# Eight row buffers, an addition ahead of the transposes and one store a chunk in the last stage of a two-layer model

## The chip, the cores and the metric

The kernel runs on one core of a Trainium2 chip. The metric is the time of one execution on the device, in microseconds (us); lower is better. Before the change three runs gave 2809.3, 2803.34 and 2809.07 us, median 2809.07. The core has five engines that run on their own and meet at semaphores: TensorE (PE: matmuls and transposes into PSUM), VectorE (DVE), ScalarE (ACT), GpSimd (POOL: here also indirect DMAs) and SyncE (SP: here the queue that issues nearly all plain DMAs).

## What is computed

The input is x, 64 sequences of 64 tokens with 256 features, 4096 tokens in all. Two layers add to it four times: a conditioned scan with attention, a quantized feed-forward, an RNN with a Mamba block, and last two mixtures of experts, one behind the other. The last term is what matters here:

```python
def _L1_ffn_ref(x, Wg, W1, W2, W3):
    xt = x.reshape(B * S, D)
    scores = xt @ Wg.T
    topk_scores, topk_idx = jax.lax.top_k(scores, TOP_K)      # 2 of 8 experts
    gate = jax.nn.silu(jnp.einsum('td,ehd->teh', xt, W1))
    up = jnp.einsum('td,ehd->teh', xt, W2)
    y = jnp.einsum('teh,edh->ted', gate * up, W3)
    ...
    out = jnp.einsum('te,ted->td', w, y)                      # sum of a token's two results
    return out.reshape(B, S, D)
...
x = x + _L1_ffn_ref(_L1_cond2_ref(...), L1_ffn_Wg, L1_ffn_W1, L1_ffn_W2, L1_ffn_W3)
```

Each token goes to two of eight experts, the results are weighted and added, and the sum is added to the residual x.

## The kernel before

The kernel keeps features on the 128 partitions (two blocks k of 128) and tokens along the free axis, and works in 8 chunks of 512 tokens (`NCH`, `CH`, `TT` = 4 groups of 128 tokens to a chunk).

The mixtures (function `mixtures`) don't compute all experts for all tokens. A gate chooses two experts for every token of a chunk (`Gate.chunk`, `Gate.lot`), and the token's row, 256 features and four tags, is sent by eight indirect DMAs a chunk (`Routing.send`, L1320, on POOL's queue) into the two experts' regions of a DRAM table. Expert tiles of 256 or 128 rows are then read back (`Routing.read`, L1328) with the expert's weights (L1520), both issued on SP. For the last mixture these are the tiles of class `Swiglu`, with two tiles loaded ahead and three buffers. A tile transposes its rows (L1534, copied by VectorE at L1536), makes the inner activations (matmuls L1661 and L1669, ScalarE L1664 and L1672, VectorE L1665 and L1674), multiplies by the last matrix (L1559), scales by the gate (ScalarE L1561), and gives each row's result to the place of its token and choice in another DRAM table, `ffn_y`, by indirect DMAs (`Routing.give`, L1335). VectorE takes a tile's tags apart in some small operations that begin at L1539. Its matmul outputs use four PSUM banks of one tag in rotation. After the gate's last chunk VectorE makes the tables that tell SP which rows and experts the remaining tiles are (`Routing.tiles`, from L1391 on).

In the last stage all results lie in `ffn_y`, two rows for each token. `Routing.fetch` (L1344) reads those of a chunk, 1 MiB, into a tile of 128 partitions x 4 groups x 2 results x 256 features. It waits for every indirect DMA that gave results. The residual x of the chunk lies in another tile, `x3_c`, loaded (L1993) while tiles were still running. For each of the two feature blocks TensorE transposes the eight 128x128 blocks of a chunk into one PSUM bank, and adds the second result of a token to the first there, in the accumulation (L2005). VectorE adds the bank to x (L2014), and SP stores the block (L2015), 256 KB. Rows have two buffers, `rows3_0` and `rows3_1`, and take 16 KB per partition of the pool `gx`; the eight x3 tiles take 32 KB.

A scheduler of the language's tile layer orders the instructions on each engine's queue, sets the semaphores, and gives pools their memory; a pool that is opened takes memory that earlier pools have given up, and its first writers wait for the last users. The order on SP can so change where a pool changes its size. SP issues DMAs in order: one that waits holds back those behind it.

Of the kernel before, what the change touches and what calls it, by code (L numbers as in the profile page):

```python
# [13 lines left out]
F32 = mybir.dt.float32  # L14
# [7 lines left out]
P = 128  # L22
B, L, D = 64, 64, 256
NT = B * L
CH = 512
NCH = NT // CH
KD = D // P
# [51 lines left out]
def bank(g, shape=(P, CH), dt=F32, tag="ps"):  # L79
    tag = g.tag or tag  # L80
    return g.psum.tile(list(shape), dt, tag=tag, name=tag)
# [1034 lines left out]
TT = CH // P  # L1116
# [345 lines left out]
def turns(queue):  # L1462

    while True:
        while queue and next(queue[0], END) is END:
            queue.popleft()
        yield
# [426 lines left out]
def mixtures(g, mix, x, weights, out, last, work, close):  # L1894

    nc, tc = g.nc, g.tc
    some = lambda pieces, n: deque(islice(pieces, n), 0)

    def tiles_on(tiles, n, *beside):

        at = 0
        for mark in tiles:
            n -= mark is TILE
            if n == 0:
                break  # L1910
            at += 1
            for pieces, many in beside:
                some(pieces, int(at * many) - int((at - 1) * many))

    with ExitStack() as ctx:
        pool = lambda name, bufs: ctx.enter_context(tc.tile_pool(name=name, bufs=bufs))
        p1 = pool("e1", 1)
        gate = Gate(g, p1, x)
        first, q2, q3, qy = pool("qw", Gelu.AHEAD + 1), pool("q2", 2), pool("q3", 2), pool("qy", 6)
        moe0, moe1 = mix.routings  # L1920
        n = moe0.ntl
        tables1 = []
        tiles = Gelu(g, (q2, q3, qy, first), weights[0]).run(
            [(moe0, lambda: mix.tables, n, NHT, None), (moe1, lambda: tables1[0], n, NHT, None)]
        )
        n += NHT
        next(tiles)
        others, shared = mix.rest(last, work, q3), mix.shared(NCH - 1, last, work)
        for _ in range(5):
            some(others, 1)  # L1930
            some(shared, 3)
        tiles_on(tiles, n - Gelu.AHEAD + 1, (others, 0.6), (shared, 0.8))
        some(others, None)
        some(shared, None)
        tables1.append(moe1.tiles(p1))
        close()

        pw, p2, p3, py = pool("gw", Swiglu.AHEAD + 1), pool("g2", 2), pool("g3", 3), pool("gy", 4)
        pg, close_pg = scoped(tc, "gate", side="right")
        pg2, close_pg2 = scoped(tc, "gate2", side="right", bufs=2)  # L1940

        def gates(chunks):
            got = {}

            def fetch(c):
                rows = pg.tile([P, TT, RW], F32, name=f"x2_{c % MLOT}")
                got[c] = rows, mix.fetch(c, rows[:, :, :D], pg2)

            fetch(chunks[0])

            for _ in range(4):
                yield
            for c in chunks:
                if c + 1 in chunks:
                    fetch(c + 1)
                    yield
                rows, routed = got.pop(c)
                mix.combine(rows[:, :, :D], routed)
                yield from gate.chunk(c, rows, pg, pg2)

        routing = gate.routing
        ntl = routing.ntl - EARLY
        tables2 = []
        tiles2 = Swiglu(g, (p2, p3, py, pw), weights[1]).run(
            [
                (routing, lambda: tables2[0], EARLY, 0, routing.sent),
                (routing, lambda: tables2[1], ntl, NHT, None),
            ]
        )

        tiles_on(tiles, Gelu.AHEAD + 3)
        others = gates(range(MLOT))
        sends = turns(gate.sends)
        tiles_on(tiles, n - 7, (others, 0.85), (sends, 0.42))
        some(others, None)
        some(chain.from_iterable(gate.sends), None)
        tables2.append(routing.early(p1))
        next(tiles2)
        some(tiles, None)
        others = gates(range(MLOT, NCH))  # L1980
        some(tiles2, 7)
        tiles_on(tiles2, EARLY - Swiglu.AHEAD, (others, 0.85), (sends, 0.42))
        some(others, None)
        some(chain.from_iterable(gate.sends), None)
        close_pg2()
        close_pg()
        tables2.append(routing.tiles(p1))
        px, close_px = scoped(tc, "gx", side="right")
        xs = []
        for c in range(NCH):  # L1990
            tiles_on(tiles2, 1)
            x = px.tile([P, KD, CH], F32, name=f"x3_{c}")
            nc.sync.dma_start(x, g.x[:, :, ts(c, CH)])  # L1993
            xs.append(x)
        some(tiles2, None)
        for c in range(NCH):
            rows = px.tile([P, TT, 2, D], F32, name=f"rows3_{c % 2}")
            routing.fetch(c, rows)
            x = xs[c]
            for k in range(KD):  # L2000
                po = bank(g, tag="acc")

                for t in range(TT):
                    for j in range(2):
                        nc.tensor.matmul(  # L2005
                            po[:, ts(t, P)],
                            rows[:, t, j, ts(k, P)],
                            g.ident,
                            start=(t == 0 and j == 0),
                            stop=(t == TT - 1 and j == 1),  # L2010
                            is_transpose=True,
                            skip_group_check=True,
                        )
                nc.vector.tensor_add(x[:, k, :], x[:, k, :], po)  # L2014
                nc.sync.dma_start(out[ts(k, P), ts(c, CH)], x[:, k, :])  # L2015
        close_px()


def scoped(tc, name, side=None, bufs=1):

    stack = ExitStack()
    kw = {"side": side} if side else {}
    return stack.enter_context(tc.tile_pool(name=name, bufs=bufs, **kw)), stack.close
# [3 lines left out]
def tile_adaln_attn_ffn_d2(ctx: ExitStack, tc: tile.TileContext, a: dict, out: bass.AP):  # L2027
# [49 lines left out]
    def close():  # L2077
        for one in (close_work, close_shared, close_mamba, close_hs):
            one()

    mixtures(g, mix, rows["ffn1"], weights, out, last, work, close)
    close_banks()
    close_mix()
# [79 lines left out]
```

## Time and profile before

| | |
|---|---|
| three runs | 2809.3, 2803.34, 2809.07 us |
| the profiled execution | 2806.4 us, span 2804.7 us |
| granted TensorE clock, mean of the span | 0.924 |
| busy share: PE, DVE, ACT, POOL | 84%, 64%, 49%, 47% |
| last results land in `ffn_y` | 2751.99 us |
| first fetch of rows issued, last addition ended | 2752.07, 2801.57 us |
| fetch of rows (L1344), 8 of 1024 KB, issue to landing | median 7.9 us |
| transposes (L2005), 128 | median 421 ns, weight loads 230 ns |
| addition to x (L2014), 16 of 128x512 | median 686 ns |
| store (L2015), 16 of 256 KB, issue to landing | 2.0 to 8.3 us, median 5.2 |
| loads of x3 (L1993), 8 of 512 KB | issued 2303.0 to 2338.8 us, 9.4 to 12.8 us to landing |

All times are from one execution recorded by the hardware profiler, in microseconds from the start of the span. In rows of the profile a line is named as L2005, `out<-in` are the program's tiles, `xN` counts instructions, and a bracket gives how long the engine was idle before and what released it. The chain of waits follows the work that ended last back in time. "PEld" are TensorE's weight loads, "SPq" is SP's issuing of a DMA.

### The profile page before, as it was taken

What the parts mean: (1) busy time and instruction counts of PE and PEld (TensorE: products, weight loads), DVE (VectorE), ACT (ScalarE), POOL (GpSimd) and SP (SyncE); (2) the same over time, 40 slices, a digit from 0 to 9 for tenths busy, and PEclk for the clock granted to TensorE, in tenths of its full rate; (3) what the DMA queues carried; (4) which work ended last, traced back from release to release, by engine and by line L of the source; (5) the groups of instructions that cost most, each with busy time, mean ns of one, the idle gap of its engine ahead of it and who ended that gap; (6) DMA issues with size and microseconds to landing.
All of it is one profiled execution on the core that took longest, in us unless ns stands there. A gap on an engine that the chain in (4) does not pass through costs nothing.

```text
span 2804.7 us, 34605 instructions
## 1 busy us (share of the span) xinstructions
PE 2368.8 (84%) x12072; PEld 1698.5 (61%) x12092; DVE 1783.4 (64%) x3017; ACT 1380.3 (49%) x2278; POOL 1323.8 (47%) x1158
## 2 busy tenths in 40 slices
PE   3979967998577888888778888869987999999995
PEld 3634435775245555555555555557765778888885
DVE  0467638982699889897978889883354443333332
ACT  0567627783675757676565757543332222222220
POOL 0013336540677676767586878754647341111110
PEclk9879988998768999998899899889999999999997
DMA  9999810002212122212122131314787757555545
GB/s 228 371 359 346 272 45 1 1 1 100 68 61 83 65 73 71 72 65 72 45 71 95 58 102 65 110 42 152 252 269 262 294 202 265 193 194 215 199 167 185
DMA packets 180630, 406.05 MB, mean 145 GB/s; under 512 B 24913, under 2 KB 84562, under 8 KB 175074
## 3 DMA queue, kind: packets, MB, share of 16 engines
q1 hardware_dynamic: 167010, 366.80, 38.7%
q0 software_dynamic: 13440, 36.98, 3.4%
q8 instruction: 97, 1.59, 0.2%
q14 instruction: 83, 0.68, 0.1%
HBM read 280.76 MB, written 144.98 MB: 152 GB/s over the span
## 4 chain that ended last, share of the span: by engine, by line
PE 45%; DVE 25%; issue 8%; ACT 7%; POOL 5%; DMA 3%; SPq 0%; DVEq 0%; POOLq 0%; ACTq 0%
DVE hb L1067 12%; PE ps L1661 11%; PE acc L1559 8%; PE out L446 4%; DVE hb L1069 3%; PE yp L1083 2%; PE mq L1797 2%; PE ps L1628 2%; PE mp L964 2%; DVE xc L909 2%; PE mq L1813 1%; PE acc L437 1%; PE s L412 1%; DVE h L628 1%; PE ps L1669 1%
## 5 line engine op out<-in xcount | busy, mean ns | idle before, releaser
L1028 POOL TENSOR_TENSOR hb<-dx,Bn 128x1024 f32<-128x1024 f32 x256 | 601.3, 2358 | 257.7 <-PE yp L1083 253.3
L1067 DVE TENSOR_TENSOR_SCAN hb<-dA,hb 128x512 f32<-128x512 f32 x512 | 602.5, 1208 | 32.4 <-ACT dA L1035 29.9
L1035 ACT ACTIVATE dA<-delta,A 128x504 f32<-128x504 f32 x512 | 344.4, 683 | 305.3 <-DVE hb L1067 302.7
L1083 PEld LDWEIGHTS yp<-ident,hb 128*128 128x128 f32 x2048 | 272.5, 154 | 179.2 <-issue 141.2
L1069 DVE TENSOR_TENSOR hb<-hb,cb 128x1024 f32<-128x1024 f32 x256 | 312.0, 1219 | 77.0 <-PE cb L980 59.5
L1661 PE MATMUL ps<-gxT,w 128*128 128x256 f32 (+1 forms) x1600 | 324.1, 361 | 0.8 <-DVE gxT L1536 0.8
L1083 PE MATMUL yp<-ident,hb 128*128 128x128 f32 x2048 | 307.6, 295 | 0.0
L1661 PEld LDWEIGHTS ps<-gxT,w 128*128 128x128 f32 x1600 | 276.4, 190 | 46.3 <-issue 12.4
L1797 PE MATMUL mq<-x,moe_s 128*128 128x256 f32 x896 | 254.6, 417 | 47.0 <-ACT up L1804 25.6
L1335 POOL DMA_INDIRECT ffn_y<-gy,to x72 | 69.2, 961 | 428.8 <-ACT gy L1561 416.3
L1797 PEld LDWEIGHTS mq<-x,moe_s 128*128 128x128 f32 x896 | 171.4, 207 | 109.8 <-ACT up L1804 34.1
L1665 DVE TENSOR_TENSOR gh<-gs,ps 128x256 f32<-128x256 f32 (+1 forms) x200 | 78.5, 393 | 205.3 <-ACT gs L1664 205.3
L980 PE MATMUL cb<-parts,pick 80*128 80x512 bf16 x256 | 106.5, 416 | 111.3 <-DVE hb L1069 96.5
L1559 PE MATMUL acc<-w,gh 128*128 128x256 f32 (+1 forms) x864 | 188.2, 388 | 0.0
L1664 ACT ACTIVATE gs<-ps 128x256 f32<-128x256 f32 (+1 forms) x200 | 72.4, 362 | 230.2 <-PE ps L1661 227.6
L1561 ACT ACTIVATE gy<-acc,wt 128x256 f32<-128x256 f32 x152 | 67.0, 472 | 234.1 <-PE acc L1559 229.6
L1559 PEld LDWEIGHTS acc<-w,gh 128*128 128x128 f32 (+1 forms) x864 | 145.4, 189 | 30.1 <-issue 13.4
L428 POOL TENSOR_TENSOR E<-E,z 128x1024 f32<-128x1024 f32 x32 | 61.6, 1924 | 151.9 <-DVE z L427 61.5
L446 PE MATMUL out<-oT,hs 128*128 128x512 f32 x256 | 119.5, 611 | 1.5 <-ACT oT L439 1.5
L1813 PE MATMUL mq<-moe_s,sh 128*128 128x256 f32 x448 | 114.3, 393 | 6.6 <-ACT up L1804 6.6
L1335 POOL DMA_INDIRECT moe_y<-gy,to x80 | 77.3, 966 | 68.2 <-ACT gy L1561 50.9
L1813 PEld LDWEIGHTS mq<-moe_s,sh 128*128 128x128 f32 x448 | 82.5, 194 | 40.5 <-issue 19.1
(459 smaller groups left out, 4376.6 us busy)
## 6 DMA issues: line engine op xcount, KB each, us to landing
w<-ffn_w SPq DMA_DIRECT2D x40, 2176.0 KB, 9.4
Bn<-B SPq DMA_DIRECT2D x128, 512.0 KB, 3.7
moe_x<-fill SPq DMA_DIRECT2D x130, 260.0 KB, 5.9
ffn_x<-fill SPq DMA_DIRECT2D x129, 260.0 KB, 6.0
w<-moe_w SPq DMA_DIRECT2D x48, 512.0 KB, 4.7
ffn_w<-in_ffn_W_dram SPq DMA_DIRECT2D x16, 640.0 KB, 8.3
gx<-moe_x SPq DMA_DIRECT2D x32, 260.0 KB, 5.0
gx<-ffn_x SPq DMA_DIRECT2D x32, 260.0 KB, 9.2
```

The costliest lines, as they stand in the source:

```text
L446: nc.tensor.matmul(ps, M[:, o, ts(k, P)], v.o[:, o], start=(o == 0), stop=(o == H // 2 - 1))
L980: nc.tensor.matmul(t, pick[:, n : n + 1].to_broadcast([rows, P]), v.parts, start=True, stop=True)
L1028: nc.gpsimd.tensor_mul(hb, vs[c].dx[p], Bn[:, n % NB, :].unsqueeze(1).to_broadcast([P, PI, CH]))
L1035: nc.scalar.activation(decays[s][i][:, :, 1:], seq(vs[c].delta[p][:, i, :])[:, :, 1:], AF.Exp, scale=w.A[:, p * PI + i, n : n + 1],)
L1067: ins = nc.vector.tensor_tensor_scan(h, dA[i].rearrange("p b l -> p (b l)"), h, 0.0, ALU.mult, ALU.add)
L1069: ins = nc.vector.tensor_tensor(hb, hb, cb.unsqueeze(1).to_broadcast([P, PI, CH]), ALU.mult)
L1083: nc.tensor.matmul(yp[i][:, t, :], hb[:, i, ts(t, P)], g.ident, start=(n == 0 and t == 0), stop=(n == S - 1 and t == CH // P - 1), is_tran ...
L1335: i = self.g.nc.gpsimd.indirect_dma_start(out=self.y, out_offset=bass.IndirectOffsetOnAxis(ap=to, axis=0), in_=y, in_offset=None)
L1559: nc.tensor.matmul(po[s], h, w, start=(i == 0), stop=(i == n - 1))
L1661: nc.tensor.matmul(ps[:, j, :], v.w12[:, k, ts(j * (full + 1) + i, P)], v.xT[:, k, :], start=(k == 0), stop=(k == KD - 1))
L1797: nc.tensor.matmul(ps[:, i % 2, :], w[:, k, ts(i, P)], xu[:, k, :], start=(k == 0), stop=(k == KD - 1))
L1813: nc.tensor.matmul(ps[:, t, :], h[:, i, ts(t, P)], self.s2[:, i, :], start=(i == 0), stop=(i == NS - 1))
```

## The change

The last loop leaves the pool `gx`, which keeps only the x3 tiles, and a pool of its own, `rows`, holds eight row buffers of 8 KB per partition. All eight fetches are issued ahead of the loop. In the loop VectorE adds a token's second result to its first, in place, for the whole chunk (128 x 4 x 256 elements); TensorE then makes four plain transposes for each feature block instead of eight accumulated ones; VectorE adds the bank to x as before; and one store of 512 KB takes both feature blocks.

```diff
-        for c in range(NCH):
-            rows = px.tile([P, TT, 2, D], F32, name=f"rows3_{c % 2}")
-            routing.fetch(c, rows)
-            x = xs[c]
-            for k in range(KD):
-                po = bank(g, tag="acc")
-
-                for t in range(TT):
-                    for j in range(2):
-                        nc.tensor.matmul(
-                            po[:, ts(t, P)],
-                            rows[:, t, j, ts(k, P)],
-                            g.ident,
-                            start=(t == 0 and j == 0),
-                            stop=(t == TT - 1 and j == 1),
-                            is_transpose=True,
-                            skip_group_check=True,
-                        )
-                nc.vector.tensor_add(x[:, k, :], x[:, k, :], po)
-                nc.sync.dma_start(out[ts(k, P), ts(c, CH)], x[:, k, :])
-        close_px()
+    pl, close_pl = scoped(tc, "rows")
+    rows = [pl.tile([P, TT, 2, D], F32, name=f"rows3_{c}") for c in range(NCH)]
+    for c in range(NCH):
+        routing.fetch(c, rows[c])
+    for c in range(NCH):
+        x, got = xs[c], rows[c]
+        nc.vector.tensor_add(got[:, :, 0, :], got[:, :, 0, :], got[:, :, 1, :])
+        for k in range(KD):
+            po = bank(g, tag="acc")
+            for t in range(TT):
+                nc.tensor.transpose(po[:, ts(t, P)], got[:, t, 0, ts(k, P)], g.ident)
+            nc.vector.tensor_add(x[:, k, :], x[:, k, :], po)
+        nc.sync.dma_start(out.rearrange("(k p) t -> p k t", p=P)[:, :, ts(c, CH)], x)
+    close_pl()
+    close_px()
```

## The prediction

> **What bounds the kernel now.** I read the page first, for the span, then the chain of waits over the end, the timeline of the end, and the timeline around 2290 us, where the built order of the two kernels differs as well. The whole-kernel shares (PE 45% of the chain) say nothing about this stage; its own rows do.
>
> ```profile
> 2749.59 2.40 DMA ffn_y<-gy,to
> ...
> 2752.07 5.51 DMA rows<-ffn_y
> 2757.58 0.14 issue
> 2757.72 6.41 PE acc L2005 x32
> ...
> 2797.19 3.66 PE acc L2005 x16
> 2800.85 0.02 issue
> 2800.88 0.69 DVE x L2014
> ```
>
> This is the chain of waits (start, length, what). Once the last scattered results have landed at 2751.99, everything to the end of the span (2804.7) is the loop that is changed: 52.7 us. Fetches of rows (7.3 us for the fetch of the last chunk, issued at 2789.76) and their 16 transposes take turns: with two buffers, fetch c+2 is issued only when chunk c's transposes have read its buffer. So the stage is a latency loop, not a full link: its windows show TensorE busy 26.6 us, VectorE 11.0, and DMA 71% with 239 GB/s.
>
> ```profile
> 2778.78 1.94 PE L2005 MATMUL acc<-ident,rows 128*128 128x128 f32 x16 [2.37 <-DMA rows<-ffn_y]
> ...
> 2797.19 3.65 PE L2005 MATMUL acc<-ident,rows 128*128 128x128 f32 x16 [4.07 <-DMA rows<-ffn_y]
> 2799.17 0.69 DVE L2014 TENSOR_TENSOR x<-x,acc 128x512 f32<-128x512 f32 x1 [5.32 <-PE acc L2005]
> 2800.88 0.69 DVE L2014 TENSOR_TENSOR x<-x,acc 128x512 f32<-128x512 f32 x1 [1.02 <-PE acc L2005]
> ```
>
> The timeline (start, length, engine, line, work). A chunk's 16 transposes take 3.65 us, or 1.94 when the TensorE clock is full, which happened for one chunk in six after the first two. The two additions that end it take 0.69 us each; from the end of the last one (2801.57) to the end of the span are 3.1 us: store, landing, closing.
>
> ```profile
> 2277.16 0.35 SPq L1520 DMA_DIRECT2D w<-ffn_w  x1
> 2277.45 0.96 POOL L1320 DMA_INDIRECT ffn_x<-x,ffn_row  x1 [0.31 <-issue]
> ...
> 2287.82 0.23 DVE L1539 TENSOR_SCALAR pick<-gx,ffn_early_rank 128x2 f32<-128x2 f32 x1 [1.02 <-DMA gx<-ffn_x]
> ...
> 2292.32 0.17 DVE L1391 COPY n_e<-ps 128x8 f32<-128x8 f32 x1 [2.13 <-PE ps L1389]
> ...
> 2299.94 0.40 DVE L1665 TENSOR_TENSOR gh<-gs,ps 128x256 f32<-128x256 f32 x1
> ...
> 2300.86 1.03 PE L1669 MATMUL ps<-gxT,w 128*128 128x256 f32 x4
> ```
>
> The second place, in Swiglu tiles that start on TensorE at 2277.0, 2292.15 and 2307.2: SP issues weights and rows for the third of them at 2277.16 and 2278.27; POOL issues the last of the eight sends of gate chunk 7 at 2277.45; VectorE waits at L1539 for these rows until 2287.82, begins the tile tables at 2292.32, and after them does the second L1665 (2299.94 to 2300.34). TensorE's L1669 at 2300.86 reuses that one's bank, so it has half a microsecond to spare.
>
> [...] with two fetches of 1 MiB in flight from 2752.07 the first landed at 2757.58, when about 1.3 of 2.1 MB had moved by the DMA view. [...] the trace's L1840, the same addition of rows with the same stride, has a median of 1224 ns.
>
> **The change, part by part.**
>
> *Fetches.* All eight are issued from 2752.07 on; in the built order only the first waits, for the results and for earlier loads that are long in. With some 0.45 us of issue each, SP is through by 2756 and the link limits. Reads alone ran at 360 to 410 GB/s here; at 395, 1 MiB takes 2.65 us. Fetch c lands at 2757.58 + 2.65c, the last at 2776.1.
>
> *Addition.* Eight new VectorE instructions, 128x1024, at 1.22: 9.8 us. They now stand between landing and transposes, on the path.
>
> *Transposes.* 8 instead of 16 per chunk. At the slow clock, by the rows: 8 before the first addition took 2757.72 to 2759.75, 2.03 us; 4 would take 3 x 0.23 + 0.42 = 1.11.
>
> *A chunk then.* The order on VectorE is: addition of rows c, x of k=0, x of k=1, addition of rows c+1 (only chunk 1's addition stands ahead of chunk 0's last). Nothing overlaps across chunks: TensorE waits for the addition, VectorE for the transposes. Period: 1.22 + 0.14 (release to transposes, as after a landing in the chain) + 2.03 (all 8 transposes; the k=0 addition fits beneath the second four) + 0.69 + 0.03 = 4.1 us. That is more than 2.65, so from chunk 2 on the fetches are hidden and this chain sets the pace.
>
> *The sum.* Rows 0 land 2757.6; addition to 2758.9; k=0 transposed at 2760.2, added to 2760.8; rows 1 (landed 2760.3) added to 2762.1; chunk 1 ends at 2764.9. Six periods of 4.1: 2789.5. The last store is now 512 KB instead of 256: 0.65 us more at 400 GB/s, so 3.8 from last addition to end: 2793.3. The stores stand behind the fetches in the ring, but from 2776.1 on they have the link alone: seven of them, 3.7 MB, need 9.4 us and are paced by the chunks, so none is waiting at 2789.5. Eight stores fewer save SP eight issues of 0.33 us, which nothing waits for: it idles between them. Without upstream effects the span is 2793.4, **11.3 us less**.
>
> *Moved loads.* The pool of x3 shrinks from 48 to 32 KB per partition, and the built order places its eight loads elsewhere on SP: x3 0 to 2 directly ahead of the weights that were issued at 2277.16, x3 3 to 7 after their rows. x3 0 waits for all eight sends of gate chunk 7, since it takes their memory. The last send, 2277.45, lands 2.4 us after its start: 2279.9. Behind this wait on SP stand those weights and rows. With 1.5 us for three issues, weights go out near 2282.2, rows near 2283.1. In the ring stand 1.57 + 2.23 + 0.27 = 4.07 MB from 2280.1: 10.4 us at 390 GB/s and 3.2 for start and landing: rows land at 2293.7 instead of 2287.8. TensorE needs them only at 2301.7 and the weights at 2307.2, but VectorE waits at L1539. That now stands after L1674 and the gxT copy, so this tile isn't held; the tables behind it are: 1.2 us of small operations, start at 2294.9 instead of 2292.32, second L1665 done 2.6 later, at 2302.9. L1669 waits from 2300.86: **2.1 us lost**. The next weights go out when the tables are made, 2.6 later, and are needed at 2322.3: covered by a whole tile. x3 3 to 7 (2.6 MB, 6.7 us) are through by about 2300.
>
> Net: -11.3 + 2.1 = -9.2 us. Span 2804.7 becomes 2795.5; the profiled execution's time 2806.4 becomes 2797.2. The median of the runs shown, 2809.07, lies 2.7 above that execution, so by it 2799.9.
>
> **Bounds of what the trace doesn't show.** TensorE's clock in the new pattern: busy 2.0 of 4.1 us; before, even 7.3 busy of 8.2 us (2784.9 to 2793.1) stayed slow. I take slow; at the full clock 8 transposes take about 1.1, a period is 3.2, and the end 5.6 us earlier. Rate with eight fetches in flight: any above 250 GB/s leaves 4.1 per chunk. Moved loads: 0 (rows land by 2291.6) to 4.5 (they land at 2296).
>
> **Rivals.**
> *The link bounds:* VectorE and TensorE keep up, and 12.6 MB in a row at 390 GB/s end near 2787. It needs a period of 2.65; additions alone take 2.6, and the built order has no addition ahead of the previous chunk's. At most this is the full-clock case: 5.6 us better, 2794. For it: one chunk of before ran fast.
> *Fetches share the rings:* eight in flight advance together, and rows 0 land only with the rest. Against it: 1.3 of 2.1 MB above. If they did, rows 0 land near 2776, and eight periods and the end follow: 2776 + 33 + 4 = 2813, +2.1 upstream, about 10 us slower than before: 2819. It decides from a landing of rows 0 at 2766.8 on, 9.2 us later than now.
> *Upstream loses more:* rows at L1539 land after 2296, or the shifted tables also delay the tile after: 4 to 7 us lost instead of 2.1, 2802 to 2805.
> *The change doesn't do what it says:* fetches wait for memory. The built order shows no wait on fetches 1 to 7.
>
> **How the numbers follow.** The chain as summed: 0.60, 2797 to 2803. Full clock in some or all chunks: 0.16, 2794 to 2797. Upstream loses more, or a slower chunk: 0.16, 2803 to 2807. Shared rings or another mishap: 0.08, above 2809. 0.2% is 5.6 us, about what a measurement of this kernel can tell from no change; faster means below 2803.5. That holds all of the first two and a little of the third: 0.79 faster, 0.14 same, 0.07 slower. Range 2794 to 2806.
>
> **What would show it.** Right: eight fetches issued within 4 us; rows landing every 2.6 to 2.8 us; additions of rows 4.1 us apart from chunk 2 on, with TensorE waiting for VectorE and not for DMA; 3.8 us after the last addition; VectorE's L1539 waiting for rows until about 2293.7 and L1669 starting near 2303. Wrong: additions of rows waiting for DMA, transposes 0.11 us apart, or L1669 on time.

## The result and the profile after

| | before | after |
|---|---|---|
| median of 16 runs each, same chip | 2807.98 us (2802.69 to 2818.86) | 2799.72 us (2792.67 to 2805.3) |
| ratio after to before, 95% interval | | 0.9976 (0.9967 to 0.9985) |
| profiled execution, span | 2806.4, 2804.7 us | 2797.36, 2795.5 us |
| last results landed, to the end of the span | 2751.99, 52.7 us | 2755.04, 40.5 us |
| DMA and VectorE busy in that stretch | 71%, 11.0 us | 84%, 20.1 us |

The kernel is faster by 0.24% (0.15 to 0.33%). The span is 9.2 us shorter: the stretch from the last landing to the end ("the loop" from here on) lost 12.2 us, and 3.1 us of that were given back ahead of it, since the last results landed 3.1 us later.

The chain of waits over the end of the kernel after (start, length, what):

```profile
2752.65 2.39 DMA ffn_y<-gy,to
...
2755.49 5.65 DMA rows<-ffn_y
...
2761.26 1.24 DVE rows L2002
...
2762.54 1.13 PE acc L2006 x4
...
2790.98 0.69 DVE x L2007
```

From the landing at 2755.04 the first fetch was on its way at 2755.49, and its rows had landed at 2761.14. Then no DMA stands in the chain any more: it is one of TensorE and VectorE, up to the last addition's end at 2790.98 + 0.69 = 2791.67, which is 3.8 us before the end.

The timeline of the same stretch shows one chunk (2768.18 to 2772.08):

```profile
2755.49 13.19 SPq L1344 DMA_DIRECT2D rows<-ffn_y  x8
...
2768.18 1.22 DVE L2002 TENSOR_TENSOR rows<-rows 128x1024 f32<-128x1024 f32 x1
2768.78 23.28 SPq L2008 DMA_DIRECT2D out_dram<-x  x8
...
2769.50 1.94 PE L2006 MATMUL acc<-ident,rows 128*128 128x128 f32 x8 [1.96 <-issue]
2770.62 0.69 DVE L2007 TENSOR_TENSOR x<-x,acc 128x512 f32<-128x512 f32 x1 [1.22 <-PE acc L2006]
2771.48 0.69 DVE L2007 TENSOR_TENSOR x<-x,acc 128x512 f32<-128x512 f32 x1 [0.16 <-PE acc L2006]
2772.08 1.22 DVE L2002 TENSOR_TENSOR rows<-rows 128x1024 f32<-128x1024 f32 x1
```

Addition of rows 1.22 us, the first transpose 0.10 after it, eight transposes 1.94 (sixteen fit into that at the full clock, as the row of before at 2778.78 shows), last addition to x, and the next addition of rows: 3.90 us from one to the next, and the same in all later chunks. No addition of rows after chunk 0 has a DMA behind its wait. The profile puts TensorE's 1.96 us of idle time down to "issue", that is, to nothing that it can see; that it is the addition on VectorE is read from the start of the transposes 0.10 us behind it in every chunk from chunk 2 on, and experiment 5 tests it. The stores (third line) begin only at 2768.78, though chunk 0's last addition to x had ended at 2766.11: SP was issuing fetches for 13.2 us (first line), and a store stands behind them in its order. The line of the fetches in the view of L1344 has min, median and max of the issue in ns:

```profile
L1344 SPq DMA_DIRECT2D rows<-ffn_y x8: 382/1732/2950, 2755.5 to 2766.1; - x8
```

In the kernel before, the same issue had a median of 380 ns.

The place upstream, timeline after:

```profile
2276.19 0.96 POOL L1320 DMA_INDIRECT ffn_x<-x,ffn_row  x1 [0.30 <-issue]
...
2280.14 1.40 SPq L1993 DMA_DIRECT2D x<-x_mid  x3
...
2282.14 0.35 SPq L1520 DMA_DIRECT2D w<-ffn_w  x1
2282.99 0.38 SPq L1328 DMA_DIRECT2D gx<-ffn_x  x1
...
2293.45 0.23 DVE L1539 TENSOR_SCALAR pick<-gx,ffn_early_rank 128x2 f32<-128x2 f32 x1 [6.13 <-DMA gx<-ffn_x]
...
2294.38 0.16 DVE L1391 COPY n_e<-ps 128x8 f32<-128x8 f32 x1
...
2301.72 0.41 DVE L1665 TENSOR_TENSOR gh<-gs,ps 128x256 f32<-128x256 f32 x1
...
2302.18 2.08 PE L1669 MATMUL ps<-gxT,w 128*128 128x256 f32 x4 [2.40 <-DVE gh L1665]
...
2304.05 1.06 PE L1534 MATMUL ps<-ident,gx 128*128 128x128 f32 x4
...
2304.90 5.43 PE L1559 MATMUL acc<-w,gh 128*128 128x256 f32 x24
...
2310.26 8.90 PE L1661 MATMUL ps<-gxT,w 128*128 128x256 f32 x40
```

The first line is the last of the eight sends for which the loads of x3 wait. These loads went out ahead of the weights, weights and rows 5 us later than before, VectorE waited for the rows until 2293.45, its tables followed at 2294.38, and the L1665 that frees a bank for L1669 ended at 2302.13. TensorE waited 2.40 us. This line and the next two hold what came on top: L1669 took 2.08 us instead of 1.03, L1534 1.06 instead of 0.60 and L1559 5.43 instead of 5.12, the values of the tile before it. The tile after started at 2310.26. A tile without a wait is 15.06 us here, and this one started at 2290.89, so 4.3 us were lost: 2.4 by the wait, 1.9 by the slow clock after it.

### The profile page after: what moved, and what is told of

It reads as the page before. It is cut to its first block, busy times and chain, and to the rows that moved or that the text cites. A ratio compares the mean times of both kernels' runs of the same rounds, so it can differ in the third digit from the quotient of the medians.

```text
span 2795.5 us, 34495 instructions
## 1 busy us (share of the span) xinstructions
PE 2359.3 (84%) x12028; PEld 1687.7 (60%) x12028; DVE 1792.2 (64%) x3025; ACT 1380.8 (49%) x2278; POOL 1320.7 (47%) x1158
## 4 chain that ended last, share of the span: by engine, by line
PE 44%; DVE 26%; issue 9%; ACT 8%; POOL 5%; DMA 3%; SPq 0%; DVEq 0%; POOLq 0%; ACTq 0%
DVE hb L1067 12%; PE ps L1661 10%; PE acc L1559 8%; PE out L446 4%; DVE hb L1069 3%; PE mq L1797 2%; PE ps L1628 2%; PE yp L1083 2%; DVE xc L909 2%; PE mp L964 2%; POOL hb L1028 1%; PE mq L1813 1%; ACT dA L1035 1%; DVE h L628 1%; PE acc L437 1%
## 5 line engine op out<-in xcount | busy, mean ns | idle before, releaser
L1665 DVE TENSOR_TENSOR gh<-gs,ps 128x256 f32<-128x256 f32 (+1 forms) x200 | 78.5, 393 | 207.7 <-ACT gs L1664 207.7
L1559 PE MATMUL acc<-w,gh 128*128 128x256 f32 (+1 forms) x864 | 188.5, 388 | 0.0
L1559 PEld LDWEIGHTS acc<-w,gh 128*128 128x128 f32 (+1 forms) x864 | 145.8, 190 | 30.2 <-issue 13.4
```

The source lines that it names most:

```text
L1559: nc.tensor.matmul(po[s], h, w, start=(i == 0), stop=(i == n - 1))
```

## The experiments

My theory after this result: the loop gains because fetches no longer wait for transposes to free a buffer, and by nothing else in the change; what sets its pace is then the back and forth of VectorE and TensorE; and the shifted loads take a third of it back. Rivals: half the transposes or fewer stores make the gain; the link is the bound already; the loss upstream is only the slow clock's scatter.

Experiments 1 to 4 ran on one chip, where the kernel before has a median of 2853.61 us (60 runs), and 5 to 8 on another, where it has 2813.75 (24 runs). Ratios are within a chip; the loop is always taken from the last results' landing to the end of the span. Line numbers are each kernel's own.

### 1. The change with the x3 loads in their old place

```diff
         xs = []
+        px.tile([P, 2, TT, 2, D], F32, name="pad")
```

The unused tile gives the pool `gx` back its 48 KB.

> The change, but the pool gx keeps its old 48 KB per partition (an unused tile), so that the loads of x3 stand on SP where they stood before. My theory, two terms: the last loop gives about 12.2 us and the moved loads take about 4.3 (2.4 of waiting at L1669, the rest a slower TensorE clock after it). Then the wait at L1669 behind the tables is gone, the loop from the last landing of results to the end of the span stays at 40.5 us, and the ratio to before is 0.9957 (12 us less). Rival: the later end of the tiles in the changed kernel's trace is scatter between executions and the moved loads cost nothing that lasts; then this runs like the change, 0.997 to 0.9976.

Measured: 2840.55 us (7 runs), ratio 0.9959 (0.9943 to 0.9974), loop 40.5 us, as in the change. The timeline at the tile concerned:

```profile
2353.86 0.41 DVE L1665 TENSOR_TENSOR gh<-gs,ps 128x256 f32<-128x256 f32 x1
...
2354.78 1.03 PE L1669 MATMUL ps<-gxT,w 128*128 128x256 f32 x4
...
2356.08 5.12 PE L1559 MATMUL acc<-w,gh 128*128 128x256 f32 x24
```

L1665 ends half a microsecond before L1669 starts, no wait is shown, L1669 takes 1.03 us, and the tile after starts 15.06 us after this one. The interval of the ratio still touches the rival's 0.997 to 0.9976, so it is the trace that decides. The whole of the loop's gain stands without the loss upstream.

### 2. The moved loads alone

```diff
+    pl, close_pl = scoped(tc, "rows")
...
-            rows = px.tile([P, TT, 2, D], F32, name=f"rows3_{c % 2}")
+            rows = pl.tile([P, TT, 2, D], F32, name=f"rows3_{c % 2}")
```

This diff and the next are excerpts, against the kernel before and with indentation ignored. The loop is that of before, with its two buffers, but these lie in a pool `pl` of their own, so `gx` shrinks and the loads of x3 move.

> The loop of before (two buffers, accumulated transposes, two stores a chunk), but its two row buffers lie in a pool of their own, so that gx shrinks to 32 KB and the loads of x3 are issued as early as in the change. My theory: the loop stays at 52.7 us, L1669 behind the tables waits 2.4 us for VectorE and TensorE is slow for some matmuls after it, 4.3 us lost, ratio 1.0015. Rival (the loads cost nothing): 1.000, no wait at L1669.

Measured: 2859.94 us (22 runs), ratio 1.0019 (1.0006 to 1.0033): slower. The timeline:

```profile
2348.95 0.23 DVE L1539 TENSOR_SCALAR pick<-gx,ffn_early_rank 128x2 f32<-128x2 f32 x1 [7.17 <-DMA gx<-ffn_x]
...
2357.69 1.19 PE L1669 MATMUL ps<-gxT,w 128*128 128x256 f32 x4 [2.77 <-DVE gh L1665]
...
2358.67 1.06 PE L1534 MATMUL ps<-ident,gx 128*128 128x128 f32 x4
...
2359.53 6.36 PE L1559 MATMUL acc<-w,gh 128*128 128x256 f32 x24
```

The same wait for rows, then TensorE stands 2.77 us for L1665, and L1534 and L1559 run slow (1.06 and 6.36 instead of 0.60 and 5.12). With 0.41 us of an earlier wait, the tile after starts 5.4 us late. So the smaller pool alone, with no change to the work, costs 5.4 us in this trace and 1.7 to 9.4 us by the interval, where the change lost 4.3. (The loop took 48.3 us here, with the code of before: its TensorE clock averaged 0.73 there against 0.64 in the profiled execution of before, where it took 52.7. The same loop can differ by 4.4 us from one execution to another; TensorE was busy 23.1 us of it here and 26.6 us there.)

### 3. Eight buffers alone

```diff
+    pl, close_pl = scoped(tc, "rows")
+    got = [pl.tile([P, TT, 2, D], F32, name=f"rows3_{c}") for c in range(NCH)]
+    for c in range(NCH):
+        routing.fetch(c, got[c])
     for c in range(NCH):
-        rows = px.tile([P, TT, 2, D], F32, name=f"rows3_{c % 2}")
-        routing.fetch(c, rows)
+        rows = got[c]
```

Accumulated transposes, sixteen a chunk, and two stores a chunk, as before; no addition of rows; the unused tile of experiment 1.

> Eight buffers and all fetches at once alone: 16 accumulated transposes a chunk and two stores of 256 KB as before, no addition of rows on VectorE, gx padded to its old size. My theory: the gain of the loop is the end of fetches and transposes taking turns. Then TensorE sets the pace, 3.65 us a chunk at the slow clock: 5.7 + 8 x 3.7 + 0.7 + 3.1 = 39 us instead of 52.7, ratio 0.995; if it gets the full clock, fetches set the pace at 2.75 and the loop takes about 33, ratio 0.993. Rival: the gain comes from half as many transposes and fewer stores; then the loop stays near 50 us, ratio 0.999.

Measured: 2839.55 us (22 runs), ratio 0.9957 (0.9941 to 0.9972), loop 37.8 us, 2.7 shorter than the change's. The timeline:

```profile
2791.97 14.29 SPq L1344 DMA_DIRECT2D rows<-ffn_y  x8
...
2804.59 1.94 PE L2009 MATMUL acc<-ident,rows 128*128 128x128 f32 x16 [1.64 <-DMA rows<-ffn_y]
...
2806.37 17.66 SPq L2019 DMA_DIRECT2D out_dram<-x  x16
...
2807.30 1.94 PE L2009 MATMUL acc<-ident,rows 128*128 128x128 f32 x16 [0.77 <-DVE x L2018]
...
2820.08 0.69 DVE L2018 TENSOR_TENSOR x<-x,acc 128x512 f32<-128x512 f32 x1 [0.18 <-PE acc L2009]
```

Sixteen transposes take 1.94 us, the full clock: TensorE went through the first two chunks without a pause (5.15 us), and the later ones follow 2.71 us from one to the next (2804.59, 2807.30), with a wait of 0.77 us for the addition to x. The last addition ends at 2820.77, but the span only at 2829.3, 8.5 us later: stores had first gone out at 2806.37, behind 14.3 us of issuing fetches. The same kernel's windows (stretch, length, busy time of PE, PEld, DVE, ACT and POOL, granted clock, DMA share, GB/s):

```profile
2814.00:2821.00 7.00, 4.54 (x39) 3.88 (x36) 3.96 (x6) 0.00 (x0) 0.00 (x0) 1.00 1.05 399
2821.00:2829.30 8.30, 0.00 (x0) 0.00 (x0) 0.00 (x0) 0.00 (x0) 0.00 (x0) 0.72 0.67 257
```

The first is at the full clock, with the link at 399 GB/s until the transposes are done; only then it falls off. So the addition on VectorE, the halved transposes and the single store aren't where the gain came from; with eight buffers the loop that has them is 2.7 us longer, in one trace each. Eight buffers and the issue of all fetches ahead of the loop come together in every run here: what each gives by itself, or three or four buffers, was not tried.

### 4. The change's loop with two buffers

```diff
-    rows = [pl.tile([P, TT, 2, D], F32, name=f"rows3_{c}") for c in range(NCH)]
-    for c in range(NCH):
-        routing.fetch(c, rows[c])
     for c in range(NCH):
-        x, got = xs[c], rows[c]
+            got = px.tile([P, TT, 2, D], F32, name=f"rows3_{c % 2}")
+            routing.fetch(c, got)
+            x = xs[c]
```

The excerpt is against the change, with indentation ignored; the stores and the additions are the change's.

> The change's loop (rows added on VectorE, half the transposes, one store a chunk) with two row buffers in gx, each fetch in the loop as before; the loads of x3 stand where they stood before. My theory: a buffer is held for 1.2 + 2.0 us instead of 3.65 and a fetch still takes over 5 us from issue to landing, so they take turns as before: 50 to 53 us, ratio 0.999 to 1.0. Rival (additions, transposes and stores bring the gain): about 41 us, ratio 0.996.

Measured: 2854.67 us (22 runs), ratio 1.0001 (0.9987 to 1.0016): no difference, loop 51.1 us. Additions of rows 2 to 4 in its timeline:

```profile
2808.38 1.23 DVE L2000 TENSOR_TENSOR rows<-rows 128x1024 f32<-128x1024 f32 x1 [2.24 <-DMA rows<-ffn_y]
...
2814.02 1.23 DVE L2000 TENSOR_TENSOR rows<-rows 128x1024 f32<-128x1024 f32 x1 [1.64 <-DMA rows<-ffn_y]
...
2819.11 1.23 DVE L2000 TENSOR_TENSOR rows<-rows 128x1024 f32<-128x1024 f32 x1 [1.10 <-DMA rows<-ffn_y]
```

Each waits for its fetch, 5.1 to 5.6 us from one to the next (the three that follow come 4.2, 9.3 and 3.9 us apart, and only the last of them waits for no DMA). Everything of the change but the eight buffers and the early issue is worth nothing that can be measured: by the interval between 3.7 us less and 4.6 us more.

### 5. The next chunk's rows added while this one is transposed

```diff
+    def both(c):
+        if c < NCH:
+            return nc.vector.tensor_add(rows[c][:, :, 0, :], rows[c][:, :, 0, :], rows[c][:, :, 1, :])
+    both(0)
     for c in range(NCH):
...
+        ahead = both(c + 1)
         for k in range(KD):
-            nc.vector.tensor_add(x[:, k, :], x[:, k, :], po)
+            i = nc.vector.tensor_add(x[:, k, :], x[:, k, :], pos[k])
+            if ahead:
+                tc.add_manual_dep(i.ins, ahead.ins.name, order, reason="behind the next chunk's rows")
```

The last line only fixes the order of the two instructions on VectorE. The unused tile is there too.

> The change, with the loads of x3 left where the kernel before has them, and on VectorE the addition of the next chunk's rows put ahead of this chunk's two additions to x. Theory: the changed loop is bound by one chain that goes back and forth between VectorE and TensorE, 3.90 us a chunk (addition 1.22, its release 0.07, transposes 1.95, last addition 0.69, less what overlaps). With the next addition made while TensorE transposes, a chunk costs the larger of VectorE's own work (1.22 + 2 x 0.69 = 2.6 us) and of the link's 2.65 us: additions of rows about 2.7 us apart, and then the stores are what ends last, as with eight buffers alone: loop of 36 to 39 us, ratio to before 0.994 to 0.9965. Rival: the chain isn't the bound, since the two results of a chunk still meet on VectorE or the fetches set the pace: additions stay 3.9 us apart, loop 40.5 us, ratio 0.996 as with the padded change.

Measured: 2797.61 us (7 runs) against 2813.75, ratio 0.9937 (0.9914 to 0.996), loop 37.9 us. The timeline:

```profile
2769.87 17.27 SPq L2020 DMA_DIRECT2D out_dram<-x  x8
2770.73 1.23 DVE L2006 TENSOR_TENSOR rows<-rows 128x1024 f32<-128x1024 f32 x1 [0.29 <-DMA rows<-ffn_y]
2771.88 1.28 DVE L2017 TENSOR_TENSOR x<-x,acc 128x512 f32<-128x512 f32 x2
...
2772.06 1.94 PE L2014 MATMUL acc<-ident,rows 128*128 128x128 f32 x8 [0.77 <-PE acc L2014]
2773.43 1.23 DVE L2006 TENSOR_TENSOR rows<-rows 128x1024 f32<-128x1024 f32 x1 [0.28 <-DMA rows<-ffn_y]
...
2786.06 0.69 DVE L2017 TENSOR_TENSOR x<-x,acc 128x512 f32<-128x512 f32 x1 [0.16 <-PE acc L2014]
```

Additions of rows are 2.70 us apart (2770.73, 2773.43), as expected, and now each waits for its DMA, 0.2 to 0.3 us in most chunks and 1.53 in one: this is the pace at which rows land, with a DMA share of 0.98 and 362 GB/s from 2756.5 to 2786.7. The slow clock (mean 0.51 over the loop) no longer matters, since 1.94 us of transposes fit into 2.70. The last addition ends at 2786.75, 30.7 us after the last landing instead of 36.6, but the span ends 7.3 us after it instead of 3.8: more than half of the 6.0 us is spent waiting for stores. The chain was the bound of the change, and the link is the next one, 2.6 us behind it by these two traces. By the ratio this is the fastest of the complete kernels here, with an interval that overlaps those of experiments 1 and 3.

### 6. Half the stores left out

```diff
-            nc.sync.dma_start(out[ts(k, P), ts(c, CH)], x[:, k, :])
+            if k == 1:
+                nc.sync.dma_start(out[ts(k, P), ts(c, CH)], x[:, k, :])
```

To experiment 3; the output's first 128 features stay unwritten.

> Eight buffers alone (transposes accumulated as before, no addition of rows on VectorE, loads of x3 where before has them), and the first feature block of every chunk isn't stored: half of the output stays unwritten, 2.1 MB less. Theory: with eight buffers alone the loop ends on the link (8.4 MB in, 4.2 MB out, near 395 GB/s), 8.5 us after the last addition; 2.1 MB less end it 5 us earlier, so the loop is 33 us instead of 37.8, and the last addition is followed by 3.1 to 4 us. Rival: the stores trail for another reason (their issue is late because the fetches hold SP, or each takes long by itself): the last one still lands 7 to 8 us after the last addition, loop 36 to 38 us.

Measured: loop 32.7 us (2763.84 to 2796.5), 5.1 less than experiment 3 for 2.1 MB less, which is 5.4 us at 390 GB/s (experiment 3's windows have 387 to 399). Ratio 0.9925 (0.9898 to 0.9953). The first fetches and the last addition in its timeline:

```profile
2764.29 14.32 SPq L1344 DMA_DIRECT2D rows<-ffn_y  x8
...
2792.42 0.69 DVE L2018 TENSOR_TENSOR x<-x,acc 128x512 f32<-128x512 f32 x1 [0.18 <-PE acc L2009]
```

The end follows that addition by 3.4 us instead of 8.5, though SP was held by the fetches as long as in experiment 3 (14.3 us). So it was the stores still to be moved, not the late issue, that kept experiment 3's end. Half the bytes are also half as many stores; the two weren't told apart, though the 5.1 us fit the bytes.

### 7. The stores on ScalarE's queue

```diff
-            nc.sync.dma_start(out[ts(k, P), ts(c, CH)], x[:, k, :])
+            nc.scalar.dma_start(out[ts(k, P), ts(c, CH)], x[:, k, :])
```

To experiment 3.

> Eight buffers alone, with the stores issued by ScalarE, which has nothing else to do there, instead of by SP behind the eight fetches. Theory: the link is the bound, and the first store goes out about 6.5 us earlier, but takes its share of the link from the fetches: the loop gains 0 to 2 us over eight buffers alone (37.8), ratio to before 0.9945 to 0.996. Rival: SP, held for some 13 to 14 us by the eight fetches, is what delays the end: stores flow from the first addition on, and the loop falls by 4 us or more, to 33 or 34 us.

Measured: 2801.17 us (11 runs), ratio 0.9959 (0.9938 to 0.998), loop 39.0 us: 1.2 longer than experiment 3, where I had expected 0 to 2 us of gain. The timeline:

```profile
2758.08 20.86 SPq L1344 DMA_DIRECT2D rows<-ffn_y  x8
...
2766.52 27.28 ACTq L2019 DMA_DIRECT2D out_dram<-x  x16
...
2779.57 3.58 PE L2009 MATMUL acc<-ident,rows 128*128 128x128 f32 x16 [2.92 <-DMA rows<-ffn_y]
...
2790.77 1.94 PE L2009 MATMUL acc<-ident,rows 128*128 128x128 f32 x16 [2.49 <-DMA rows<-ffn_y]
...
2792.75 0.69 DVE L2018 TENSOR_TENSOR x<-x,acc 128x512 f32<-128x512 f32 x1 [0.18 <-PE acc L2009]
```

Stores start right behind the first addition (2766.52) and the span ends 3.2 us behind the last one. But what they take of the link the fetches lack: SP now needs 20.9 us from the first of these to the last, where experiment 3 took 14.3, and transposes wait for rows, as at 2779.57, where behind 2.92 us of waiting the sixteen also ran at the slow clock (3.58 us instead of 1.94). So neither experiment 6 nor experiment 7 shows a cost of the held SP by itself; in experiment 7 one could still be hidden, since there the fetches went out later as well.

### 8. The change again

> The change itself beside the others on the same chip: loop 40.5 us, 12 us less than before, and 4 to 5 us lost at the tile behind the moved loads; ratio to before 0.9965 to 0.998, 4 to 5 us slower than with those loads left in place, and at least 4 us slower than eight buffers alone.

Measured: 2804.17 us (12 runs) against 2813.75, ratio 0.9965 (0.9949 to 0.9981); loop 40.3 us. The timeline at the tile upstream:

```profile
2301.31 0.23 DVE L1539 TENSOR_SCALAR pick<-gx,ffn_early_rank 128x2 f32<-128x2 f32 x1 [5.72 <-DMA gx<-ffn_x]
...
2310.05 1.13 PE L1669 MATMUL ps<-gxT,w 128*128 128x256 f32 x4 [2.00 <-DVE gh L1665]
...
2311.46 5.12 PE L1559 MATMUL acc<-w,gh 128*128 128x256 f32 x24
```

TensorE waits 2.00 us, and here the clock stays: 1.13 and 5.12 us. This tile began at 2299.17 and the next at 2316.50, which is 2.3 us lost where I had expected 4 to 5. Eight buffers alone, which the expectation names, weren't run on this chip. The change is 6.6 us slower than experiment 5 by the medians, and 3.0 slower than experiment 7, the only one with accumulated transposes on this chip that stores everything. On the chip of experiments 1 to 4 the padded change and eight buffers alone are within each other's intervals, so that their loops differ by 2.7 us is read from one trace each and not from the times.

## Why the prediction was right, and where not

The predicted time, 2799.9, lies beside the median of 2799.72, and the span is 2795.5 as forecast. That precision is luck in part. The sum was -11.3 + 2.1; the trace has -12.2 + 4.3, and 1.3 us that the same tile upstream happened to start earlier (2290.89 instead of 2292.15; this is scatter, since the order of the work ahead of it is the same but for a few neighbours). Without that last term it is -7.9, which agrees with the runs: medians 8.3 apart, 4.2 to 9.3 us by the ratio. The -12.2 also hangs on the one execution of before in which the loop took 52.7 us; against the 48.3 us that the same loop took in experiment 2 it would be -7.8. The loop of the change took 40.3 to 40.5 us in all three of its traces (one of them with the padding), and experiment 1, which has the gain without the loss, is 11.7 us faster by its ratio (7.4 to 16.3).

*What bounds the kernel* (a latency loop over two buffers, not a full link): right. Experiment 4 keeps the two buffers and gains nothing; experiments 3 and 1 show that eight, all fetched ahead, give it all.

*First rows:* forecast 5.6 us after the last landing, measured 6.1. Seven waits on SP ahead of the first fetch, 0.06 us each, now stand in the chain (2755.06 to 2755.49), where before had one.

*The chain that sets the pace:* right, with TensorE waiting for VectorE from chunk 2 on. The period was put at 4.1 us and is 3.90. The step from addition to transposes is 0.10 us instead of 0.14, eight transposes up to the start of the last addition are 1.98 (2769.50 to 2771.48) instead of 2.03, and the next addition of rows starts 0.09 before the previous addition ends (2771.48 + 0.69 against 2772.08). Six periods are 1.2 us shorter for that, and the first two chunks 0.3 longer: the loop's 0.9. Experiment 5 turned the order on VectorE around, and the period fell to 2.70, the rate of the landings.

*TensorE slow:* right for the change (1.94 to 1.97 us for eight, in all chunks): TensorE never worked for more than 1.97 us in a row, and its clock never rose (0.50 in the windows from 2758 to 2791.7).

*"SP is through by 2756":* wrong, and with it the sign that eight fetches are issued within 4 us. SP was held until 2768.7: the first three issues took 0.38 to 0.51 us each, the fourth 1.15, the last four 2.3 to 2.95, and in experiment 7, where stores shared the link, the eight took 20.9 us from first to last. What holds an issue that long was not shown. It did no harm, for stores have slack in this chain: at 2768.78 two chunks were done (the third store, issued at 2772.67, took 11.5 us and landed at 2784.20, behind the last fetch at 2780.42), and by the end the last store stood alone, 2.7 us from issue to landing, with the 3.8 us that were forecast.

*Moved loads:* the path was right, and its times agree in part by luck. Rows were forecast at L1539 for 2293.7 and came at 2293.45; tables 2294.9, came 2294.38; L1669 near 2303, came 2302.18. But the tile and the sends ran 1.3 us earlier in this execution than in that of before: the last send started at 2276.19, not 2277.45. Against the start of the tile the rows came after 2.6 us (2290.89 to 2293.45), where 1.5 was forecast, because the first load of x3 went out 4.0 us behind the start of the last send (3.8 in experiment 8, 3.1 in experiment 2) and not 2.7; the tables then took 0.5 us less than forecast. So the wait came out at 2.40, near the 2.1.

The loss was mis-sized: 2.1 us forecast, 4.3 measured in the profiled execution, 5.4 in experiment 2, 2.3 in experiment 8. The term left out is the TensorE clock after the stall: where the wait was 2.40 or 2.77 us, the work behind it ran slow for about 3 us; where it was 2.00, not. Windows of the change (the first two lines) and of experiment 8 (the third), columns as in experiment 3:

```profile
2298.71:2302.13 3.42, 1.06 (x5) 0.58 (x4) 3.42 (x24) 0.00 (x0) 0.00 (x0) 1.00 0.16 60
2302.13:2305.54 3.41, 3.36 (x10) 2.81 (x11) 1.94 (x8) 0.76 (x2) 0.00 (x0) 0.50 0.52 102
...
2308.18:2311.60 3.42, 1.55 (x9) 1.40 (x10) 2.99 (x19) 0.76 (x2) 0.00 (x0) 1.00 0.00 0
```

In the traces of before and of the change the recorded clock changes in steps of 3.41 us, and the first two windows are such steps. In the change the wait left TensorE busy 1.06 us of one step, and the next step was slow; in experiment 8 it was busy 1.55 us of the window with the wait, and behind it (from 2311.60) the clock stayed full: L1559 took 5.12 us.

*The rivals.* The link bounds: not in the change, but 2.6 us behind it, as experiments 5 and 6 show. Shared rings: refuted, rows 0 landed 6.1 us after the last results, at 2761.14, when five fetches of 1 MiB had been issued and SP was busy with the sixth. Upstream loses more: the 4 to 7 us that this rival names were lost in two traces of three, but not by its mechanism, for in the change the rows came before 2296 and the rest was the clock.

## What to carry to other kernels

Where fetches and the work on them take turns over two buffers, more buffers with all fetches ahead can give the whole gain; an edit of the work itself that comes in the same change has to be judged with the buffers already there. Here the loop with it was 2.7 us longer than without it, in one trace each and not in the times, and as short as that only once the addition was put a chunk ahead. When the transfers are no longer the latency, ask for the order of instructions on the engine that two steps share, since putting the next item's first step ahead of this item's last took 1.2 us off each 3.9. And a pool that changes its size can move loads that lie far ahead of the edit (here 470 us ahead of the loop, by 23 us and more), so that a wait of theirs holds up what stands behind them: read the built order of every queue there, and price a stall of TensorE with the clock it can lose as well (here 1.9 us more behind a wait of 2.40, 0.3 behind one of 2.00).

## What the hardware showed that was not expected

- SP, with eight loads of 1 MiB in a row, was held 13.2 us in the change (median 1.73 us an issue) and 14.3 in experiment 3, and took 20.9 from the first to the last where stores on another queue shared the link. With at most two in flight before, an issue took 0.38 us in the median.
- In the traces of before and of the change the recorded TensorE clock is 1.00 or 0.50 and keeps each value, the last of a record apart, for a multiple of 3.413 us: it changes only at the edges of steps of that length, which lie elsewhere in each of the two. The length of a pause didn't decide alone: the one of 2.40 us in the change, which left TensorE busy 31% of one step, lost the clock; one of 2.49 us (experiment 7, at 2790.77) didn't, and the sixteen transposes behind it took 1.94 us.
- The full clock held with nothing but transposes: sixteen in 1.94 us out of each 2.71 us in experiment 3, with a granted clock of 1.00 in its windows from 2806 to 2821, where TensorE was busy 10.2 of 15 us. It had risen while TensorE went through the first two chunks without a pause (mean 0.82 from 2797.8 to 2806). In experiment 5, with 1.94 to 1.97 us of transposes to a chunk 2.7 us apart, the mean of the loop is 0.51. In the traces of before and of the change every rise (49 and 46) follows a step with TensorE busy 85% or more, though not every such step brings one, and the full clock was kept behind steps of down to 42%. Most falls (40 of 50 and 38 of 47) follow steps under half, but some follow fuller ones, so this isn't the whole rule.
- The loop of before took 52.7 us in one trace and 48.3 in another (experiment 2), with TensorE busy 26.6 and 23.1 us and a mean clock of 0.64 and 0.73.
